# A graph network on one core: the attention's last 1130 targets move from matrix products to gathered rows

## The chip, the cores and the metric

The kernel runs on one core of a Trainium2 chip. A core has five engines that work beside each other and take their instructions in order, each from its own queue: PE (TensorE, matrix products), DVE (VectorE), ACT (ScalarE), POOL (GpSimd) and SP (SyncE, which here only issues DMAs). GpSimd also issues DMAs, the indirect ones, in which a list of row numbers says which rows of a table come in. The metric is the device time of one launch in microseconds (us), lower is better; the figure for a kernel is the median of its runs.

## The reference

Four layers act on 6250 nodes of 128 features and 206,250 edges; each layer's output is added to its input and normalised over the features. `src` and `dst` are the ends of an edge, and the edges are sorted by `dst`.

```python
x = layernorm(x + L0(x))   # x @ Ws.T + bs + mean over a node's edges of x[src] @ Wn.T + bn
x = layernorm(x + L1(x))   # relu([x[src], edge_attr] @ W1 + b1) @ W2 + b2, mean per dst, then a two-layer MLP per node
x = layernorm(x + L2(x))   # x_comb = [x, sum of edge_attr @ We + be]; x_comb + sum of x_comb[src]; a two-layer MLP
x = layernorm(x + L3(x))   # attention, below
# L3, with 4 heads of 32 features and n = 6250; a loop edge from each node to itself is added
h = (x @ W).reshape(n, 4, 32)
a_src, a_dst = (h * att_src).sum(-1), (h * att_dst).sum(-1)
e = exp(leaky_relu(a_src[src] + a_dst[dst], 0.2) - max over the edges of dst)
out = segment_sum(h[src] * e[..., None], dst) / segment_sum(e, dst)
x3 = relu(layernorm(out.reshape(n, 128) + bias, gamma, beta))
```

## The kernel before

Nodes are held 128 to a partition block: `NB` = 49 blocks, the last of 106 rows. `groups` are the 13 runs of up to four blocks (512 nodes, the last of 106), `duos` the 25 runs of two. The program is written out in one order by hand (a manual schedule): each engine executes its instructions in the order in which the Python code issues them, so a generator that is advanced step by step (`yield`) puts its pieces between those of the main loop. There are four stages.

**dense0** makes the adjacency matrix. For two blocks of targets at a time, GpSimd gathers each target's stretch of the sorted edge list: 64 slots of `dst` and of `src` (`search`, `find`, lines 831 to 860). `sort` (line 862) marks the slots whose `dst` is the target itself (`mine`). DVE compares them with counters (`onehots`, line 891, bf16), PE multiplies the comparisons, and the counts go to `A` and from there to a table `adj` in DRAM (line 1007), for all later stages. `prepare_chunks` (line 275) loads all of `src` and `dst` into `src_i` and `dst_r`, 147 chunks of 128 x 11 edges that stay in SBUF.

**mlp** (line 1054) runs layer 1 over the edges, 441 units of up to 4 x 128 edges. For each, SP loads edge features (line 1069), GpSimd gathers the rows of `t1` by columns of `src_i` (line 127 by way of line 1073), PE multiplies (lines 1093 and 1107), and `onehot` (line 782) compares `dst_r` with a counter once a chunk.

**dense2** (line 1012) does layer 2 with `adj`, 25 rounds of 147 products. SP loads each round's piece of `adj` in five DMAs (line 1027) as buffers come free. `node2` (line 494), advanced by one step every ten products, finishes a duo of the round before: it leaves the projected features `hs` in `acc` and the attention's two scalars per node and head in `al`.

**attend** (line 1134) does layer 3 as products with `adj` too. exp of a leaky ReLU of a sum is one of two products of a factor per source and a factor per target, and a comparison chooses which. The 13 groups make six `units`: five of two groups (1024 targets), and a sixth of two groups plus the last 106 targets (`more`, lines 1147 to 1149). For each head and unit a loop of 25 iterations passes over the sources, two blocks an iteration: 4 x 6 x 25 = 600 iterations. In an iteration SP loads the piece of `adj` that is needed three iterations later (line 1283), ACT makes the comparison `r` for two blocks (line 1320), DVE takes `B = min(A, r)` and `C = A - B` in bf16 (lines 1327 and 1329), and PE adds ten products of 512 columns to the sums (line 1347). The sixth unit also has the products of line 1349, and the DVE operations of lines 1333 and 1334, for its 106 extra targets.

Around the loop, lanes advance generators. A `Lane` (line 1253) lets one generator take a step at every second iteration: `sums` closes the last unit (`close`, line 1224) and transposes the next unit's targets; `ends` normalises and stores finished groups in the last head (`finish3`, line 615); `news` makes the next head's source tables (`tables`, line 1185) from the second unit of a head on. `tables` splits an f32 into three bf16 parts: ACT copies (line 1196), GpSimd subtracts (line 1198), ACT copies the rest, GpSimd subtracts again, ACT copies. For the first head the same is done in the first unit, two groups ahead of need.

Of the kernel before, what the change touches and what calls it, by code (L numbers as in the profile page):

```python
# [9 lines left out]
F32 = mybir.dt.float32  # L10
BF16 = mybir.dt.bfloat16
I32 = mybir.dt.int32
# [6 lines left out]
P = 128  # L19
# [49 lines left out]
def kernel(  # L69
# [38 lines left out]
    dram = ctx.enter_context(tc.tile_pool(name="dram", bufs=1, space=bass.MemoryType.DRAM))  # L108
    setup = ctx.enter_context(ExitStack())
# [8 lines left out]
    t3 = dram.tile([N, HW], F32)  # L118
    t3d = dram.tile([N + W, 2 * HEADS], F32)
# [24 lines left out]
    src_i = const.tile([P, NCH, T], I32)  # L144
    dst_r = const.tile([P, NCH, T], F32)
# [128 lines left out]

    def prepare_chunks(prep, pps):

        dst_i = dst_r.bitcast(I32)
        nc.vector.memset(src_i[:, NCH - 1, :], 0)
        nc.vector.memset(dst_i[:, NCH - 1, :], -1)
        for to, of in ((dst_i, dst), (src_i, src)):  # L280
            if NF:
                nc.sync.dma_start(to[:, :NF, :], of[: NF * P * T].rearrange("(c p t) -> p c t", p=P, t=T))
            if tail:
                nc.sync.dma_start(to[:tail, NF, :], of[NF * P * T :].rearrange("(p t) -> p t", t=T))
# [25 lines left out]
        nc.vector.tensor_sub(dst_r, dst_r, w0b.unsqueeze(2).to_broadcast([P, NCH, T]))  # L310
# [183 lines left out]
    def node2(acc, al, pool, pps, n0, rows, nb, G=4, hT=None):  # L494
# [32 lines left out]
        if not keep:  # L527
            nc.vector.tensor_copy(hs[:rows, :nb, D:], al[:rows, 0, b0 : b0 + nb, :])
            store(t3, hs, n0, rows, nb)
# [103 lines left out]
    def general():  # L633
        with ExitStack() as st:
            gp = st.enter_context(tc.tile_pool(name="gacc", bufs=1))
            acc = gp.tile([P, 3, NA], F32, name="gacc")
            for k in range(3):
# [4 lines left out]
                           allow_small_or_imprecise_dtypes=True)  # L642
            row_i = gp.tile([P, NCH], I32, name="row_i")
# [3 lines left out]
            def edges(name, rows_of):  # L647
                with tc.tile_pool(name=f"{name}s", bufs=1) as ep, \
# [5 lines left out]
                    nc.vector.tensor_copy(node, dst_r[:, ds(c, 1), :].rearrange("p c t -> p (c t)"))  # L654
                    w0 = ep.tile([P, 1], F32, name="w0")
                    nc.vector.tensor_copy(w0, w0b[:, ds(c, 1)])
                    ri = ep.tile([P, 1], I32, name="ri")
                    nc.vector.tensor_copy(ri, row_i[:, ds(c, 1)])
                    nc.vector.tensor_scalar(node, node, w0, None, op0=ALU.add)
# [96 lines left out]
    def fast():  # L756
# [24 lines left out]

        def onehot(ep, c, bufs=2):
            K = sizes[c]
            oh = ep.tile([P, T, W], F32, name="oh", bufs=bufs)
            nc.vector.tensor_tensor(
                oh[:K], iota[:K, :W].unsqueeze(1).to_broadcast([K, T, W]),
                dst_r[:K, c, :].unsqueeze(2).to_broadcast([K, T, W]), ALU.is_equal)
            return oh
# [11 lines left out]
        def dense0(stack):  # L800
# [21 lines left out]
            with tc.tile_pool(name="d0o", bufs=1) as one, tc.tile_pool(name="d0", bufs=1) as ep, \  # L822
# [39 lines left out]
                def sort(sb):  # L862
# [5 lines left out]
                    nc.vector.tensor_reduce(degc[:, 2 * sb : 2 * sb + 2], mine, AX.X, ALU.add)  # L868
                    low = ep.tile([P, 2, S], I32, name="low")
# [94 lines left out]
                for sb in range(NS + 1):  # L964
# [5 lines left out]
                    for i in range(STEPS):  # L970
                        g = sb * STEPS + i
                        if g == 2:
                            flush_dma(nc.sync)

# [79 lines left out]
        def mlp(name, node, pool, pps):  # L1054
# [4 lines left out]
            with tc.tile_pool(name=f"{name}e", bufs=1) as ep, \  # L1059
# [5 lines left out]
                def load(i):  # L1065
# [5 lines left out]
                    g[i] = ep.tile([P, U, H], F32, name="g1", bufs=AHEAD + 1)  # L1071
                    for t in range(k):
                        gather(g[i][:K, t, :], t1, src_i[:, c, :], a + t, K)
# [60 lines left out]
        def attend(acc, al):  # L1134


            M = 3 * (CH + 1)
# [8 lines left out]

            units = [(g[0][0], g, []) for g in (groups[k : k + 2] for k in range(0, len(groups), 2))]
            if len(units) > 1 and len(units[-1][1]) == 1 and units[-1][1][0][2] == 1:
                units[-2][2].extend(units.pop()[1])
            with tc.tile_pool(name="f3c", bufs=1) as one, tc.tile_pool(name="f3", bufs=2) as ep, \  # L1150
# [22 lines left out]
                s = one.tile([P, NB, HEADS], F32, name="s")  # L1173
# [3 lines left out]
                nc.scalar.activation(vs, vs, AF.Exp)  # L1177

# [28 lines left out]
                def targets(k, h, n0, of, more):  # L1207

                    to = one.tile([P, 2 * F + P], F32, name=f"ad{k % 2}")
                    last = None  # L1210
                    for m0, rows, nb in of + more:
# [12 lines left out]
                def close(h, of, s):  # L1224

                    sT = []
                    for (m0, rows, nb), sums in zip(of, s):
                        sT.append(ep.tile([M, 2, F], F32, name="sT") if rows * nb > P else one.tile([M, 2, P], F32, name="sTm"))
                        nc.scalar.copy(sT[-1][:, 0, : rows * nb], sums[0])
# [22 lines left out]

                class Lane:


                    def __init__(self):
                        self.left, self.due = [], 0
# [4 lines left out]
                    def step(self, now):  # L1262
                        if self.left and now >= self.due:
# [3 lines left out]
                            self.due = now if lag is self else now + (lag or 2)  # L1267
# [5 lines left out]
                A, more_of, ready = {}, {}, {}  # L1273
                steps = [(h, *u) for h in range(HEADS) for u in units]
                work = [(h, n0, of, more, a) for h, n0, of, more in steps for a in range(0, NB, 2)]

                def load(i):
                    if i < len(work):
                        h, n0, of, more, a = work[i]
# [5 lines left out]
                        if more:  # L1285
                            more_of[i] = ep.tile([P, 2, 2 * P], BF16, name="Am", bufs=4)
                            nc.sync.dma_start(more_of[i][:, :n].rearrange("p l q -> p (l q)"),
                                              adj[more[0][0] // (2 * P), :, a * 2 * P : (a + n) * 2 * P])

                sums, news, ends = Lane(), Lane(), Lane()  # L1290
# [3 lines left out]
                first = [tables(0, groups[k::2]) for k in range(2)]  # L1294
                made, i, now = 0, 0, 0
                for k, (h, n0, of, more) in enumerate(steps):
                    ad, n, m = ready.pop(k), width(of), width(more)
                    tab, minus = tabs[h % 2]
                    s = [[sps.tile([P, F], F32, name="s") for g in of] for _ in range(2)]
                    sm = rps.tile([P, 2, P], F32, name="sm") if more else None  # L1300
# [9 lines left out]
                    for b in range(0, NB, 2):  # L1310
# [5 lines left out]
                        At, Am = A.pop(i), more_of.pop(i, None)  # L1316
                        i += 1
                        r = ep.tile([P, 2, 2 * F + P], BF16, name="r")
                        for l in range(kk):
                            nc.scalar.activation(r[:, l, : n + m], ad[:, : n + m], AF.Relu,  # L1320
                                                 bias=bias[:, b + l, h : h + 1], scale=BIG)
# [9 lines left out]
                        if more:  # L1331
                            bm = ep.tile([P, 3, P], BF16, name="Bm")
                            nc.vector.tensor_tensor(bm[:, :kk, :m], Am[:, :kk, :m], r[:, :kk, n : n + m], ALU.min)
                            nc.vector.tensor_sub(bm[:, 2, :m], Am[:, 0, :m], bm[:, 0, :m])
                        terms = [(0, tab[:, b, 0], lambda c0, c1: bt[:, 0, c0:c1], lambda: bm[:, 0, :m])]
                        if kk == 2:
                            terms += [
                                (0, tab[:, b + 1, 0], lambda c0, c1: bt[:, 1, c0:c1], lambda: bm[:, 1, :m]),
                                (1, minus[:, b // 2], lambda c0, c1: bt[:, 1, c0:c1], lambda: bm[:, 1, :m]),
                                (1, tab[:, b + 1, 1], lambda c0, c1: At[:, c0 // w : c1 // w, 1, :w], lambda: Am[:, 1, :m])]  # L1340
                        terms.append((1, tab[:, b, 1], lambda c0, c1: ct[:, c0:c1], lambda: bm[:, 2, :m]))
# [75 lines left out]
```

## Time and profile before

| | |
|---|---|
| median of 3 runs | 4996.36 us (4988.17 to 5003.37) |
| the profiled execution's own time | 5474.87 us, of which the span is 5473.1 us |
| mean granted TensorE clock in it | 0.942 |
| busy in the span: PE, DVE, ACT, POOL | 91%, 55%, 47%, 36% |
| first attention product of line 1347 to the last | 3886 to 5407 us of the span |
| 0 to 848 us, GpSimd's first gather of layer 1 | dense0, at 848.7 us |
| layer 1's gathers | 848.7 to 3396 us, 1617 of them |

The profile is of one execution, which took 9.6% longer than the median; times in it are compared with its own span. "Busy" counts the time in which an engine executes; a busy PE is not PE at its peak, and pieces of work on one engine overlap a little. The page's second part cuts the span into 40 slices of 137 us, one digit each, in tenths. In a group's row the columns are: source line, engine, operation, output and inputs, their shapes, the count, the busy time in us, the mean of one in ns, and the idle time before them with what ended it. A row of the timeline has the start in us, the duration in us, the engine, the line, and the idle time before it in brackets.

### The profile page before, as it was taken

The numbers are of one execution on the slowest core, as the hardware profiler recorded it, in microseconds if no ns is written. First come the engines' busy times: TensorE is split into PE (matmuls) and PEld (weight loads), VectorE is DVE, ScalarE is ACT, GpSimd is POOL, SyncE is SP. The second block draws the span as 40 slices with busy tenths as digits, with TensorE's granted clock in tenths as the row PEclk, the third lists the DMA queues.
The fourth block names the chain that finished last, engine by engine and source line by source line (L and its number), as shares of the span: only waits on it lengthen the run. The fifth ranks groups of instructions, "written<-read, shape, count | busy, mean of one in ns | idle before, by whom it ended". The sixth has DMA issues, their size and how long they took to land. (4 is left out here: it accounts for less than half of the span.)

```text
span 5473.1 us, 90752 instructions
## 1 busy us (share of the span) xinstructions
PE 4978.6 (91%) x33855; PEld 4095.8 (75%) x33855; DVE 3007.3 (55%) x5084; ACT 2592.4 (47%) x3617; POOL 1989.4 (36%) x1966
## 2 busy tenths in 40 slices
PE   4999998998998999988999999999699999999995
PEld 3999997887888888888888888899455555555553
DVE  6888873233333333332333333222488888888998
ACT  3444442233323333332323323100599899999884
POOL 3333325666666666666666665000110010010000
PEclk9999998899998998998998988999899999999997
DMA  6333324444444444444444443555377777777773
GB/s 120 121 133 133 139 114 137 125 128 126 126 125 124 123 124 125 125 126 124 127 124 126 128 125 99 191 187 188 115 216 217 220 217 226 215 214 227 211 212 116
DMA packets 599589, 834.35 MB, mean 152 GB/s; under 512 B 119837, under 2 KB 484313, under 8 KB 594917
## 3 DMA queue, kind: packets, MB, share of 16 engines
q1 hardware_dynamic: 513077, 603.59, 36.3%
q0 software_dynamic: 85072, 224.21, 14.3%
q8 instruction: 272, 4.46, 0.3%
q14 instruction: 176, 1.44, 0.1%
q10 hardware_dynamic: 992, 0.66, 0.1%
HBM read 738.23 MB, written 89.88 MB: 151 GB/s over the span
## 5 line engine op out<-in xcount | busy, mean ns | idle before, releaser
L127 POOL DMA_INDIRECT g<-t,src_i x1617 | 1570.4, 971 | 986.8 <-issue 785.7
L1320 ACT ACTIVATE r<-ad,bias 128x1024 bf16<-128x1024 f32 (+1 forms) x1176 | 1276.7, 1155 | 91.6 <-DVE B L1327 57.6
L1095 DVE TENSOR_TENSOR g<-g,pre 128x512 f32<-128x512 f32 x882 | 548.0, 640 | 1320.3 <-issue 339.6
L1347 PEld LDWEIGHTS <-acc 128*99 128x99 bf16 x5856 | 698.1, 126 | 606.7 <-issue 157.7
L1107 PE MATMUL seg<-oh,g 128*128 128x64 f32 (+1 forms) x6468 | 1036.5, 284 | 44.4 <-issue 42.2
L1107 PEld LDWEIGHTS seg<-oh,g 128*128 128x128 f32 (+1 forms) x6468 | 959.3, 205 | 82.4 <-issue 48.6
L1093 PE MATMUL pre<-W1s,eaT 128*128 128x256 f32 (+1 forms) x3234 | 892.5, 417 | 115.5 <-DVE g L1095 57.3
L1347 PE MATMUL s<-B,acc 128*99 128x512 bf16 x3504 | 885.4, 382 | 89.4 <-DVE B L1327 84.0
L1096 ACT ACTIVATE g<-g 128x512 f32<-128x512 f32 x882 | 506.2, 592 | 681.8 <-DVE g L1095 478.9
L1093 PEld LDWEIGHTS pre<-W1s,eaT 128*128 128x128 f32 (+1 forms) x3234 | 634.8, 209 | 244.9 <-issue 110.6
L1327 DVE TENSOR_TENSOR B<-A,r 128x2048 bf16<-128x2048 bf16 x600 | 723.2, 1205 | 119.8 <-ACT r L1320 90.6
L1084 ACT COPY eaT<-tp 128x512 f32<-128x512 f32 (+1 forms) x441 | 240.7, 546 | 1067.7 <-PE pre L1093 316.5
L1107 PE MATMUL seg<-oh,ea 128*128 128x64 f32 (+1 forms) x3234 | 664.7, 287 | 32.2 <-issue 31.3
L1107 PEld LDWEIGHTS seg<-oh,ea 128*128 128x128 f32 (+1 forms) x3234 | 528.3, 204 | 32.8 <-issue 32.2
L907 ACT CAST A<-pa 128x784 bf16<-128x784 f32 x400 | 324.5, 811 | 349.2 <-PE pa L904 320.3
L798 PE MATMUL sum<-A,xs 128*128 128x256 bf16 (+1 forms) x3675 | 467.5, 273 | 0.4 <-ACT A L907 0.4
L1329 DVE TENSOR_TENSOR C<-A,B 128x1024 bf16<-128x1024 bf16 x600 | 430.4, 717 | 63.6 <-PE s L1347 0.8
L1198 POOL TENSOR_TENSOR xs<-xs,acc 128x264 f32<-128x264 f32 (+1 forms) x104 | 103.7, 1004 | 993.6 <-ACT acc L1196 972.3
L798 PE MATMUL sum<-A,acc 128*128 128x256 bf16 (+1 forms) x3675 | 409.4, 271 | 3.5 <-DMA A<-adj 3.5
L798 PEld LDWEIGHTS <-acc 128*128 128x128 bf16 x3675 | 355.2, 98 | 45.0 <-issue 5.0
L798 PEld LDWEIGHTS <-xs 128*128 128x128 bf16 x3675 | 357.6, 102 | 35.3 <-issue 0.6
L904 PE MATMUL pa<-oh,oh 128*128 128x98 bf16 x3200 | 355.8, 269 | 28.0 <-ACT A L907 23.4
(229 smaller groups left out, 4472.7 us busy)
## 6 DMA issues: line engine op xcount, KB each, us to landing
A<-adj SPq DMA_DIRECT2D x2304, 128.0 KB
ea<-in_edge_attr_dram SPq DMA_DIRECT2D x292, 256.0 KB
A<-adj SPq DMA_DIRECT2D x100, 704.0 KB
ea<-in_edge_attr_dram SPq DMA_DIRECT2D x146, 192.0 KB
g<-t,src_i POOLq DMA_INDIRECT x1617
Am<-adj SPq DMA_DIRECT2D x96, 128.0 KB
A<-adj SPq DMA_DIRECT2D x25, 320.0 KB
t<-y SPq DMA_DIRECT2D x24, 256.0 KB
```

The costliest lines, as they stand in the source:

```text
L127: nc.gpsimd.indirect_dma_start(out=to, out_offset=None, in_=table, in_offset=bass.IndirectOffsetOnAxis(ap=index[:K, t : t + 1], axis=0))
L798: nc.tensor.matmul(ps[:, :n], parts[part][:, b, :], a(b)[:, :n], start=k == 0, stop=k == 3 * NB - 1)
L904: nc.tensor.matmul(ps[:, o, q * LO : (q + 1) * LO], ohs[g][0][:, 2 * j + o, :, q], ohs[g][1][:, 2 * j + o, :, q], start=True, stop=True)
L907: nc.scalar.copy(A[sb][:, :, q0 : q0 + 2 * QI].rearrange("p k (o q) -> p k o q", q=QI), ps[:, :, : QI * LO].rearrange("p o (q k) -> p k o ...
L1093: nc.tensor.matmul(pre[:K, t, :], eaT[i][:, b + t, :K], W1s[:, 1, :], start=True, stop=True)
L1095: nc.vector.tensor_add(gb, gb, pre[:K, :n, :])
L1096: nc.scalar.activation(gb, gb, AF.Relu)
L1107: nc.tensor.matmul(ps[:, m, :], rows, oh[c][:K, a + t, :], start=a + t == 0 and m == 0, stop=a + t == T - 1, skip_group_check=True)
L1320: nc.scalar.activation(r[:, l, : n + m], ad[:, : n + m], AF.Relu, bias=bias[:, b + l, h : h + 1], scale=BIG)
L1327: nc.vector.tensor_tensor(wide(bt), At[:, :ns, :kk, :w], wide(r), ALU.min)
L1329: nc.vector.tensor_sub(ct[:, :n].rearrange("p (s q) -> p s q", q=w), At[:, :ns, 0, :w], bt[:, 0, :n].rearrange("p (s q) -> p s q", q=w))
L1347: nc.tensor.matmul(s[to][g][:M, : c1 - c0], row, rhs(c0, c1), start=to not in begun, stop=stop)
```

## The change

The attention's matrix part keeps five units (`UNITS`), the first 5120 targets: 4 x 5 x 25 = 500 iterations. The last three groups (`rest`: 512, 512 and 106 targets, nine blocks) are worked out from their slots. Four things are done for it, in this order of the program:

- dense0's `sort` writes each such block's masked source numbers and the mask to DRAM (`slot_src`, `slot_not`), five times two DMAs.
- `src` and `dst` no longer stay in SBUF for layer 1. `load_edges` brings a chunk's two columns in two small DMAs on SP's queue, six chunks ahead; `onehot` subtracts the chunk's first node first (`at`). `prepare_chunks` still loads all of `dst` for its own use, not `src`.
- `node2` in dense2 stores `hs` and the source scalar to a table `t3` of 132 columns, two DMAs a duo on SP's queue.
- `attend` gets a generator `gathered` in a lane `others`, which takes a step at every iteration. It works through 72 chunks of eight slots of one block: GpSimd gathers eight times 128 rows of `t3`, three chunks ahead of need (four buffers); then, a step each, DVE forms the logits, ACT takes exp, DVE multiplies the rows by it, and PE adds the eight slots into one PSUM tile with the identity as weights. An absent slot has 300 taken from its logit. After eight chunks DVE divides.

The sixth unit, `more` and its operations are gone. The general path, which another branch would take for other inputs, is adapted and not run here.

```diff
@@ dense0, sort
                     nc.vector.tensor_reduce(degc[:, 2 * sb : 2 * sb + 2], mine, AX.X, ALU.add)
+                    if 2 * sb + 2 > R0:
+                        k0 = 2 * sb - R0 // 2 * 2
+                        of = ep.tile([P, 2, S], I32, name="of")
+                        nc.vector.tensor_tensor(of, s, mine, ALU.mult)
+                        nc.sync.dma_start(slot_src[k0 : k0 + 2].rearrange("b p s -> p b s"), of)
+                        none = ep.tile([P, 2, S], F32, name="none")
+                        nc.vector.tensor_scalar(none, mine, -1.0, 1.0, op0=ALU.mult, op1=ALU.add)
+                        nc.sync.dma_start(slot_not[k0 : k0 + 2].rearrange("b p s -> p b s"), none)
@@ fast
+        def load_edges(c):
+
+            if c < NCH:
+                edges[c] = edge_pool.tile([P, 2, T], I32, name="edges", bufs=8)
+                for k, of in enumerate((src, dst)):
+                    nc.sync.dma_start(edges[c][: sizes[c], k, :],
+                                      of[c * P * T : c * P * T + sizes[c] * T].rearrange("(p t) -> p t", t=T))
+
         def onehot(ep, c, bufs=2):
             K = sizes[c]
+            at = ep.tile([P, T], F32, name="at", bufs=2)
+            nc.vector.tensor_scalar(at[:K], edges.pop(c)[:K, 1, :], w0b[:K, c : c + 1], None, op0=ALU.subtract)
@@ mlp, load
                     g[i] = ep.tile([P, U, H], F32, name="g1", bufs=AHEAD + 1)
+                    if a == 0:
+                        load_edges(c + 6)
                     for t in range(k):
-                        gather(g[i][:K, t, :], t1, src_i[:, c, :], a + t, K)
+                        gather(g[i][:K, t, :], t1, edges[c][:, 0, :], a + t, K)
@@ node2
-        if not keep:
+        if keep:
+            for c, of in ((slice(0, D), hs), (slice(D, HW), al[:, 0, b0 : b0 + nb, :])):
+                nc.sync.dma_start(t3[n0 : n0 + n, c].rearrange("(b p) d -> p b d", p=rows), of[:rows, :nb])
+        else:
@@ attend
-            units = [(g[0][0], g, []) for g in (groups[k : k + 2] for k in range(0, len(groups), 2))]
-            if len(units) > 1 and len(units[-1][1]) == 1 and units[-1][1][0][2] == 1:
-                units[-2][2].extend(units.pop()[1])
+            units = [(groups[2 * k][0], groups[2 * k : 2 * k + 2]) for k in range(UNITS)]
...
+                def gathered():
+
+                    Q = 8
+                    chunks = [(g, j, q) for g, (n0, rows, nb) in enumerate(rest) for j in range(nb) for q in range(0, S, Q)]
+                    rows_of, slots = {}, {}
+
+                    def issue(i):
+                        if i < len(chunks):
+                            g, j, q = chunks[i]
+                            if q == 0:
+                                k = rest[g][0] // P + j - R0 // 2 * 2
+                                slots[g, j] = [ep.tile([P, S], dt, name=name) for dt, name in ((I32, "slot"), (F32, "none"))]
+                                for t, of in zip(slots[g, j], (slot_src, slot_not)):
+                                    nc.sync.dma_start(t, of[k])
+                            rows_of[i] = ep.tile([P, Q, HW], F32, name="g3", bufs=4)
+                            for t in range(Q):
+                                gather(rows_of[i][:, t, :], t3, slots[g, j][0], q + t, P)
+
+                    for i in range(3):
+                        issue(i)
+                    yield 8
+                    for i, (g, j, q) in enumerate(chunks):
+                        issue(i + 3)
...
+                        if q == 0:
...
+                            ps = rps.tile([P, HW], F32, name="sg")
+                            nc.tensor.matmul(ps, ident, own, start=True, stop=False)
+                            yield
+                        nc.vector.tensor_add(e, e, al[:, 1, b].unsqueeze(1).to_broadcast([P, Q, HEADS]))
+                        nc.vector.scalar_tensor_tensor(e, e, SLOPE, e, op0=ALU.mult, op1=ALU.max)
+                        nc.vector.tensor_sub(e, e, less[:, q : q + Q])
+                        yield
+                        nc.scalar.activation(e, e, AF.Exp)
+                        yield
+                        xh = x[:, :, :D].rearrange("p t (h c) -> p t h c", h=HEADS)
+                        nc.vector.tensor_mul(xh, xh, e.unsqueeze(3).to_broadcast([P, Q, HEADS, CH]))
+                        yield
+                        for t in range(Q):
+                            nc.tensor.matmul(ps, ident, x[:, t, :], start=False, stop=q + t == S - 1)
+                        yield
+                        if q + Q == S:
...
+                            if j == nb - 1:
+                                ends.add(finish3(go, pool, n0, rows, nb))
+                            yield
...
-                sums, news, ends = Lane(), Lane(), Lane()
+                sums, news, ends, others = Lane(), Lane(), Lane(), Lane(1)
...
+                others.add(gathered())
...
-                        if more:
-                            bm = ep.tile([P, 3, P], BF16, name="Bm")
-                            nc.vector.tensor_tensor(bm[:, :kk, :m], Am[:, :kk, :m], r[:, :kk, n : n + m], ALU.min)
-                            nc.vector.tensor_sub(bm[:, 2, :m], Am[:, 0, :m], bm[:, 0, :m])
...
-                        for lane in (sums, news, ends):
+                        for lane in (sums, news, ends, others):
                             lane.step(now)
```

## The prediction

> **What bounds the kernel now.** I read the page's slices first, for the stages, then busy time and groups in the attention, then single instructions.
>
> ```profile
> PE   4999998998998999988999999999699999999995
> DVE  6888873233333333332333333222488888888998
> ACT  3444442233323333332323323100599899999884
> POOL 3333325666666666666666665000110010010000
> ```
> ```profile
> 3903.00:5407.00 1504.00, 1423.30 (x7228) 859.95 (x7228) 1321.55 (x1983) 1348.28 (x1424) 96.07 (x92) 0.99 0.72 213
> ```
>
> The last 11 slices are the attention. The second row is its main part, 3903 to 5407 us: stretch and sum, then PE, PEld, DVE, ACT and POOL busy, the granted clock (0.99), DMA share, GB/s. PE is busy 95% of it, ACT 90%, DVE 88%, GpSimd 6%: three engines share the bound, and GpSimd alone is free. In layer 1 (slices 6 to 24) PE is the bound and GpSimd is at 6 tenths with its gathers.
>
> ```profile
> L1320 ACT ACTIVATE r<-ad,bias 128x1024 bf16<-128x1024 f32 (+1 forms) x1176 | 1276.7, 1155 | 91.6 <-DVE B L1327 57.6
> L1347 PE MATMUL s<-B,acc 128*99 128x512 bf16 x3504 | 885.4, 382 | 89.4 <-DVE B L1327 84.0
> L1327 DVE TENSOR_TENSOR B<-A,r 128x2048 bf16<-128x2048 bf16 x600 | 723.2, 1205 | 119.8 <-ACT r L1320 90.6
> L1329 DVE TENSOR_TENSOR C<-A,B 128x1024 bf16<-128x1024 bf16 x600 | 430.4, 717 | 63.6 <-PE s L1347 0.8
> L1198 POOL TENSOR_TENSOR xs<-xs,acc 128x264 f32<-128x264 f32 (+1 forms) x104 | 103.7, 1004 | 993.6 <-ACT acc L1196 972.3
> ```
>
> Each engine waits only for its neighbour: shortening one helps little, leaving out iterations helps all. By the ACT copies of line 1229 that end each unit, a unit of 1024 targets takes 60.3 us (25 iterations of 2.41), the sixth 67.2, 67.4, 67.1 and in the last head 73.4.
>
> GpSimd's gathers come in no attention row of before, so two other places price them: layer 1, where they run back to back, and dense0, where DVE does long bf16 operations beside them. Timelines of GpSimd, then DVE, then GpSimd in dense0:
>
> ```profile
> 2001.04 0.95 POOL L127 DMA_INDIRECT g<-t,src_i  x1 [0.30 <-issue]
> 2002.30 0.95 POOL L127 DMA_INDIRECT g<-t,src_i  x1 [0.30 <-issue]
> ```
> ```profile
> 316.82 2.28 DVE L891 TENSOR_TENSOR oh<-kp,table 128x4096 bf16<-128x4096 bf16 x1
> 319.03 1.78 DVE L891 TENSOR_TENSOR oh<-kb,table 128x3136 bf16<-128x3136 bf16 x1
> ```
> ```profile
> 316.38 0.96 POOL L127 DMA_INDIRECT sup<-in_dst_dram,at  x1 [0.15 <-DVE low L870]
> 317.64 2.28 POOL L127 DMA_INDIRECT sup<-in_dst_dram,at  x1 [0.30 <-issue]
> 320.23 1.40 POOL L127 DMA_INDIRECT slots<-in_dst_dram,at  x1 [0.30 <-issue]
> ```
>
> Free, a gather takes 0.95 us plus a gap of 0.30: one per 1.25 us, of rows of 256, 1024 or 1500 bytes alike. Beside L891 it takes 2.28: it began at 317.64, DVE's operation ended at 319.10, and it ended 0.82 later, though DVE's next operation began at once. The third likewise ends 0.82 after 320.81. So a gather waits out the DVE operation that it meets, and no more.
>
> **What is removed.** Four sixth units, 67.2 + 67.4 + 67.1 + 73.4 = 275 us, with all they do on PE, ACT, DVE and SP. Attention before, from the first product (3886) to the last (5407): 1521 us.
>
> **What the new lane costs the three engines.** A chunk takes four steps, and two more for each eight chunks, so 4.25 iterations; with the first wait of eight iterations the lane is through after 8 + 72 x 4.25 = 314 of 500. PE, a chunk: eight f32 products of 132 columns. The layer-1 product of line 1093 (256 columns) comes as two records 0.216 us apart, that of line 1107 (64 columns) as two 0.112 apart; 132 columns lie near the lower, 8 x 2 x 0.112 = 1.8 us. Bounds: 0 if they fell into PE's 5% of idle time, 8 x 2 x 0.216 = 3.5. DVE: the product of 1024 f32 elements, 1.2 us (line 439's 128x1024 f32 takes 1.16), three small operations of 0.17 (line 1193), a share of the block's own: 1.8 us. ACT: one exp of 32 elements, 0.25. On engines alone a chunk takes 4.25 x 2.41 + 1.8 = 12.0 us. This is on the path.
>
> **What it costs GpSimd: the step that decides.** Eight gathers a chunk are 10.0 us free, and would hide in 12.0. But DVE is seldom idle here. In a chunk it does 4.25 times B (1.22 us in this stage) and C (0.70), and the 1.2 us product. An arrival at a random time meets an operation of length d with chance d/T and waits d/2: (4.25 x (1.22^2 + 0.70^2) + 1.2^2)/2 = 4.9, so 4.9/T us a gather, T being the chunk's time. L1198 gives the same picture: 0.67 us when free, 1.0 in the mean. T = 8 x (1.25 + 4.9/T) gives T = 13.0 us, and a gather every 1.63 us. So GpSimd, not PE, sets the pace, by 1 us a chunk.
>
> [...] I take 13.0, and keep 12.0 as the lower end.
>
> `tables` adds to it: its subtracts stand in the same queue. In the changed kernel's instruction order eight gathers lie ahead of nearly each pair. While a next head's tables are made (100 of 125 iterations), every eight iterations (1.88 chunks) bring two subtracts of 1.14 us: 1.2 us a chunk. ACT's next copy waits for the subtract, 2 x 2.41 = 4.8 us after it was issued, while eight gathers of 1.5 take 12: ACT stands some 7 us, behind it the comparisons `r`, DVE and PE. That is no loss of its own while GpSimd stays busy through it: three chunks are in hand, so DVE has its rows when ACT goes on. I allow GpSimd 0.4 us of idling a chunk: T = 11.6 + 8 x 4.9/T, T = 14.35 us.
>
> **The sum for the attention.** The first unit took 86 us (3886 to 3972), its subtracts in bursts 15 us apart. Now 24 gathers come first, 35 us, of which a burst's 15 are free: +20. Four rounds of eight gathers and four subtracts take 12 + 5 where they took 15: +8. In all 114 us, with 7 chunks gathered. Of the other 65, 50 iterations without tables hold 12, at 13.0 = 156; 53 at 14.35 = 761. The last three chunks' products: 5. By then 300 iterations are done; 200 remain, x 2.41 = 482, and 15 for the last head, whose units before took 62 to 65 us beside `finish3`. Sum: 114 + 156 + 761 + 5 + 482 + 15 = 1533, +12 on 1521.
>
> **The rest.** Tail: before, DVE finished six groups after the last product, at 9.2 us each (line 618 begins at 5416.37 and 5425.56), because `ends` takes 17.5 iterations a group. Now three groups are finished early; in the last head 100 iterations remain after its first unit, some 5.3 groups, so 4.7 are left where 5 full ones and a small one were: -9. Attention's head: a handful of DVE operations and an exp: +2. dense2: SP's queue now has two stores between a round's five loads and the next five, and they wait for `al`. DVE's line 525 ends it at 3622.9 in the round from 3610.9 to 3628.1, so all five loads wait until 5.2 us before need. Two 704 KB loads issued at 3614.9 had landed by 3618.7; the first tile should just come in time. Bounds 0 and 25 x 2 us; taken +3. Layer 1: two loads of 128 runs of 44 bytes a chunk, six chunks ahead; SP takes 0.4 us to issue each in 16, and `at` is 0.17 us on a DVE a third busy, so nothing, hidden by five units of prefetch; if a gather's index were late, PE would be next. Bounds 0 and 40. dense0: ten small DVE operations and DMAs against a load of all `src` saved, nothing.
>
> +12 - 9 + 2 + 3 = +8 us on 5473, +0.15%. The median is 0.913 of the profiled execution's 5474.87; +7 on 4996.36 gives **5004**.
>
> **Rivals.**
>
> - GpSimd keeps up (gathers free as in layer 1, or met between operations). Then 65 chunks at 12.0 = 780 replace 917, and the start is 105: 1387 in place of 1521, with the rest -138, -126 on the median: 4870. For it: GpSimd is 6% busy now. Against: dense0's rows.
> - Slower: ACT's stalls aren't covered. Each subtract of `tables` after the first head's holds ACT, and GpSimd runs dry meanwhile, because the next gathers are issued only as the lanes move on. Eight iterations then take 8 x 2.41 + 1.88 x 1.8 + 2 x 7 = 36.7 us where the sum has 27. With 5 us uncovered a stall: 32.7, times 28 such stretches: +160, so +168 and 5150. It decides against the change from about 2 us a stall. For it: 993.6 us of L1198's idle time ended by ACT shows how tight this chain is. Against: three chunks in hand.
> - The stages before pay: small loads delay layer 1 by 40 us or dense2 by 2 us a round. With the attention level, 5040. Against: no DMA is waited for long there now.
>
> **How the numbers follow.** About 0.3%, 15 us, is what can be told from no change. GpSimd sets the pace as summed: 0.45, its own range 4955 to 5050 (0.08 us a gather, from a chunk's 13.0 or 14.35 being 0.65 out, is 46 us); of it 0.15 faster, 0.11 same, 0.19 slower. GpSimd keeps up: 0.20. ACT stalls: 0.26. Earlier stages: 0.09, 0.01 of it the same. Faster 0.35, same 0.12, slower 0.53. The range, 4855 to 5140, reaches into both outer cases.
>
> **What would show it.** Gathers of the attention at 1.25 us in the mean with their gap: the first rival. At 1.5 to 1.7, with GpSimd near 90% busy for a thousand us: the sum. ACT's line 1196 copies waiting for `xs` over 5 us, with GpSimd idle just after: the second rival. Round length 17.2 us in dense2 and layer 1's 2548 us unchanged: the rest right. If f32 products of 132 columns cost more than 0.25 us, or the new loads stop SP, the prediction is wrong by something that I don't see.

## The result, and the profile after

The changed kernel takes 5191.4 us in the median of four runs (5185.31 to 5199.07), the kernel before 4995.49 in the median of four. The ratio is 1.0393, with an interval of 1.0371 to 1.0415: slower by 3.9%. The forecast was 5004, its range 4855 to 5140.

The profile of before that is shown above has to be set right first. That execution's span was 5473.1 us because its layer 1 was long: its gathers ran from 848.7 to 3396 us, and the granted clock was 0.91 from 1000 to 2800 us. In another profiled execution of the same kernel (span 4989.6, below called "before, second profile") they end at 2928, the clock there is 1.00, and the attention is as long as it was: first product at 3403.1, last at 4923.5, 1520.5 us. After the change layer 1's gathers run from 852 to 2928 us. One group of the runs below came from a chip where layer 1 took some 2570 us in each kernel profiled, where the kernel before took 5485 us, and where engines stood idle here and there with no cause in the profile; those runs are compared with each other only.

By stage, in us of the span:

| | before, second profile | after |
|---|---|---|
| layer 1, first gather to last | 2078 | 2076 |
| first attention product at | 3403.1 | 3408.7 |
| attention, first product to last | 1520.5 | 1720.1 |
| last product to the end | 66.0 | 54.5 |

So the attention lost 199.6 us, the tail gave 11.5 back, and what lies ahead cost 5.6. All of the loss is in the attention. Its slices, after (slices of 130 us, the attention from slice 27 on):

```profile
PE   4999998999999999999999999947878777779995
DVE  6888875344444444444444322246667756678898
ACT  4444443333333333333333210045556655569985
POOL 3343333777777777777777400045656665541000
PEclk9999999999999999999999999978889988989998
```

Windows of the attention of after, then of the second profile of before (stretch and sum, PE, PEld, DVE, ACT, POOL busy, granted clock, DMA share, GB/s):

```profile
3425.00:5128.00 1703.00, 1372.23 (x6758) 862.68 (x6758) 1205.80 (x1889) 1147.09 (x1296) 732.59 (x659) 0.92 0.75 173
```
```profile
3420.00:4923.00 1503.00, 1422.78 (x7227) 862.00 (x7227) 1321.70 (x1983) 1347.68 (x1423) 96.84 (x92) 0.99 0.71 213
```

Before, PE was busy 95% of this stretch, ACT 90%, DVE 88%. After, it is 81%, 67% and 71%, and GpSimd has 43%. No engine is full any more: the loss is waiting, not work. (In the rows of after the lines have moved: `r` is 1423, PE's products 1444, `B` 1429, `C` 1431, the subtract of `tables` 1241 and ACT's copy 1239, the gather's helper 135; in edited kernels they shift by two more at most.) The DMA share rises while the bytes moved per second fall, from 213 to 173. That pair is the first hint that some transfers have become dear. The groups, after:

```profile
L1423 ACT ACTIVATE r<-ad,bias 128x1024 bf16<-128x1024 f32 x980 | 1050.7, 1137 | 140.7 <-DVE B L1429 140.2
L1444 PE MATMUL s<-B,acc 128*99 128x512 bf16 x2920 | 771.6, 402 | 345.6 <-DVE B L1429 341.7 <-ACT sT L1272 1.7
L135 POOL DMA_INDIRECT g<-t,slot x576 | 673.1, 1169 | 451.0 <-issue 185.1 <-PE sg L1348 103.6 <-PE s L1444 56.1
L1429 DVE TENSOR_TENSOR B<-A,r 128x2048 bf16<-128x2048 bf16 (+1 forms) x500 | 603.7, 1207 | 435.4 <-ACT r L1423 237.0 <-DMA A<-adj 154.7 <-PE s L1444 23.9
L1431 DVE TENSOR_TENSOR C<-A,B 128x1024 bf16<-128x1024 bf16 x500 | 352.0, 704 | 52.7 <-PE s L1444 0.9 <-PE sg L1348 0.5 <-DVE B L1429 0.5
L1241 POOL TENSOR_TENSOR xs<-xs,acc 128x264 f32<-128x264 f32 (+1 forms) x104 | 80.7, 784 | 231.6 <-ACT acc L1239 209.1 <-DMA slot<-slot_src 21.7
```

`B` on DVE (line 1429) waited 120 us in all before and 435 now, and the row names the two things that end these waits: ACT's comparisons `r`, 237 us, and the loads of `adj`, 155 us. The gathers themselves are not the bound: they have 451 us of idle time, of which 185 are the gaps of 0.3 us between them. The waits from 3540 to 4450 us, where most of the gathering lies (called "the stretch" from here on; us in all, times, longest):

```profile
ACT acc L1239 <- POOL xs L1241: 200.2, 33, 13.8
PE s L1444 <- DVE B L1429: 192.8, 73, 11.5
...
DVE B L1429 <- ACT r L1423: 141.1, 47, 10.9
DVE B L1429 <- DMA A<-adj: 106.0, 33, 11.5
```

The chain reads from the top: ACT waits 33 times, 6 us each, for a GpSimd subtract of `tables`; its comparisons come late by as much, so DVE waits for `r`, and PE for DVE. Beside this runs a second chain: 33 times DVE waits for a piece of `adj`, 3.2 us each. In the same stretch of the second profile of before there were five such waits, 3.4 us together.

One place shows both. The timelines of GpSimd, ACT, DVE and PE of after (start, duration, idle time before it in brackets):

```profile
3656.33 0.68 POOL L1241 TENSOR_TENSOR xs<-xs,acc 128x264 f32<-128x264 f32 x1
...
3668.56 0.94 POOL L135 DMA_INDIRECT g<-t,slot  x1 [1.05 <-DMA g<-t,slot]
3669.51 0.68 POOL L1241 TENSOR_TENSOR xs<-xs,acc 128x264 f32<-128x264 f32 x1
3681.64 0.96 POOL L135 DMA_INDIRECT g<-t,slot  x1 [11.45 <-issue]
```
```profile
3657.04 0.42 ACT L1239 CAST acc<-xs 128x264 bf16<-128x264 f32 x1 [7.72 <-POOL xs L1241]
3657.37 2.18 ACT L1423 ACTIVATE r<-ad,bias 128x1024 bf16<-128x1024 f32 x2
```
```profile
3672.27 1.23 DVE L1429 TENSOR_TENSOR B<-A,r 128x2048 bf16<-128x2048 bf16 x1 [5.80 <-DMA A<-adj]
...
3682.87 1.29 DVE L1429 TENSOR_TENSOR B<-A,r 128x2048 bf16<-128x2048 bf16 x1 [7.37 <-DMA A<-adj]
```
```profile
3673.55 2.72 PE L1444 MATMUL s<-B,acc 128*99 128x512 bf16 x6 [4.81 <-DVE B L1429]
...
3677.77 2.13 PE L1348 MATMUL sg<-g,ident 128*128 128x132 f32 x16
3684.22 2.06 PE L1444 MATMUL s<-B,acc 128*99 128x512 bf16 x6 [4.32 <-DVE B L1429]
...
3688.49 1.46 PE L1444 MATMUL s<-B,acc 128*99 128x512 bf16 x6
```

ACT stood 7.72 us until the subtract at 3656.33 was through, and only then made its next comparisons. Then DVE stood 5.80 and 7.37 us for two loads. While everything stood, GpSimd stood too: its next gather began at 3681.64, after 11.45 us. That fits its buffer, one of four, coming free only when line 1348 had read it, at 3677.77 + 2.13 = 3679.90. And PE, after 4.81 us of idling, took 2.72 us for six products that take 1.46 in a full stream; more on that in the last section.

### The profile page after: what moved, and what is told of

It reads as the page before. It is cut to its first block, busy times and chain, and to the rows that moved or that the text cites. A ratio compares the mean times of both kernels' runs of the same rounds, so it can differ in the third digit from the quotient of the medians.

```text
span 5183.3 us, 90914 instructions
## 1 busy us (share of the span) xinstructions
PE 4660.0 (90%) x33381; PEld 3920.8 (76%) x33381; DVE 2933.1 (57%) x5116; ACT 2394.5 (46%) x3478; POOL 2653.6 (51%) x2542
## 3 DMA queue, kind: packets, MB, share of 16 engines
q0 software_dynamic: 103504, 263.17, 23.1%
q14 instruction: 186, 1.52, 0.1%
## 5 line engine op out<-in xcount | busy, mean ns | idle before, releaser
L135 POOL DMA_INDIRECT g<-t,edges x1617 | 1584.8, 980 | 502.7 <-issue 391.1
L1444 PEld LDWEIGHTS <-acc 128*99 128x99 bf16 x4880 | 639.9, 132 | 839.2 <-issue 467.7
L1423 ACT ACTIVATE r<-ad,bias 128x1024 bf16<-128x1024 f32 x980 | 1050.7, 1137 | 140.7 <-DVE B L1429 140.2
L1444 PE MATMUL s<-B,acc 128*99 128x512 bf16 x2920 | 771.6, 402 | 345.6 <-DVE B L1429 341.7
L1143 PE MATMUL seg<-oh,g 128*128 128x64 f32 (+1 forms) x6468 | 964.1, 272 | 0.0
L1143 PEld LDWEIGHTS seg<-oh,g 128*128 128x128 f32 (+1 forms) x6468 | 887.8, 192 | 24.0 <-issue 1.2
L135 POOL DMA_INDIRECT g<-t,slot x576 | 673.1, 1169 | 451.0 <-issue 185.1
L1429 DVE TENSOR_TENSOR B<-A,r 128x2048 bf16<-128x2048 bf16 (+1 forms) x500 | 603.7, 1207 | 435.4 <-ACT r L1423 237.0
L1129 PE MATMUL pre<-W1s,eaT 128*128 128x256 f32 (+1 forms) x3234 | 776.7, 381 | 20.2 <-DVE g L1131 20.2
L1431 DVE TENSOR_TENSOR C<-A,B 128x1024 bf16<-128x1024 bf16 x500 | 352.0, 704 | 52.7 <-PE s L1444 0.9
```

What stands on the lines that cost most here:

```text
L135: nc.gpsimd.indirect_dma_start(out=to, out_offset=None, in_=table, in_offset=bass.IndirectOffsetOnAxis(ap=index[:K, t : t + 1], axis=0))
L1129: nc.tensor.matmul(pre[:K, t, :], eaT[i][:, b + t, :K], W1s[:, 1, :], start=True, stop=True)
L1143: nc.tensor.matmul(ps[:, m, :], rows, oh[c][:K, a + t, :], start=a + t == 0 and m == 0, stop=a + t == T - 1, skip_group_check=True)
L1423: nc.scalar.activation(r[:, l, :n], ad[:, :n], AF.Relu, bias=bias[:, b + l, h : h + 1], scale=BIG)
L1429: nc.vector.tensor_tensor(wide(bt), At[:, :ns, :kk, :w], wide(r), ALU.min)
L1431: nc.vector.tensor_sub(ct[:, :n].rearrange("p (s q) -> p s q", q=w), At[:, :ns, 0, :w], bt[:, 0, :n].rearrange("p (s q) -> p s q", q=w))
```

## The experiments

The runs were made on several chips. Beside the first three runs the kernel before took 4999.36 us, beside the last four 4995.87, so their times are set against the 5191.4 of after; the four between them are of the chip with the long layer 1.

Two causes were to be told apart. **The queue**: `tables`' subtracts stand behind gathers in GpSimd's queue, ACT waits for them, and all wait for ACT. **The row**: absent slots have the source number 0, since `of = s * mine`, so most of the later gathers of a block fetch one row of `t3` again and again; if such packets are slow, the loads of `adj` come late behind them. The mean degree is 33 and a block has 64 slots, so the last three or four of its eight chunks are nearly all absent. The trace keeps every packet of the DMA queues; the mean of the gathers' packets (eight rows, 4224 bytes), by chunk of a block, is this in after:

```
chunk      1     2     3     4     5     6     7     8
us      0.292 0.301 0.298 0.323 0.621 1.213 1.331 1.238
```

Up to the degree a packet takes 0.30 us, beyond it four times as much.

**Absent slots keep the number of their neighbour in the edge list**

```diff
-                        of = ep.tile([P, 2, S], I32, name="of")
-                        nc.vector.tensor_tensor(of, s, mine, ALU.mult)
-                        nc.sync.dma_start(slot_src[k0 : k0 + 2].rearrange("b p s -> p b s"), of)
+                        nc.sync.dma_start(slot_src[k0 : k0 + 2].rearrange("b p s -> p b s"), s)
```

The logits of these slots have 300 taken off as before, so the same is computed.

> The changed kernel, but absent slots keep the source number that stands in the edge list there (some other target's) in place of 0; the mask takes them out as before. Hot row: all absent slots name row 0 of the table, and packets of the slots from 40 on take 1.2 us where those of the first 32 take 0.30; the loads of the adjacency wait their turn behind them. Then these packets fall to 0.30 us, units with gathers take 76 to 85 us in place of 100, the attention falls from 1720 to 1530 to 1560 us and the time from 5191 to about 5000 to 5035 us. ACT's stalls behind GpSimd (the second rival of the prediction): packets get shorter, the units do not: 5150 to 5191 us.

It took 5069.01 us, ratio 1.0149 (1.0130 to 1.0168), so 122 us less than after. The attention took 1605 us. Packets now take 0.28 to 0.31 us in all eight chunks. Their share of the DMA engines' time, after and then here, for the same count and bytes (packets, MB, share):

```profile
q0 software_dynamic: 103504, 263.17, 23.1%
```
```profile
q0 software_dynamic: 103504, 263.17, 18.9%
```

The waits here, in the same stretch:

```profile
ACT acc L1237 <- POOL xs L1239: 213.4, 30, 14.5
...
DVE B L1427 <- DMA A<-adj: 7.5, 5, 6.5
```

The waits for `adj` fall from 106.0 to 7.5 us. Nothing in the attention but the numbers of the absent rows was changed, so the row is a cause. That it acts by late loads can be read from the packets too. `adj`'s own packets (1024 bytes) take 0.054 us in the mean of the stretch in after and 0.052 here, so they are not slower; they come later. From the issue of a load to the end of its last packet pass 2.6 us in the median and 6.9 or more for a tenth of the loads in after, and 2.2 and 2.8 here (an estimate: packets are counted off in the order of the issue, 128 a load). ACT's waits for the subtracts stay as they were: 30 of 7.1 us. The gain is short of what was expected, as the second cause is still there.

**`tables`' subtracts on DVE**

```diff
-                                nc.gpsimd.tensor_sub(xs[:, :nb], xs[:, :nb], tab[:, bs, :, k, :])
+                                nc.vector.tensor_sub(xs[:, :nb], xs[:, :nb], tab[:, bs, :, k, :])
```

> The changed kernel with the subtracts of the source tables on VectorE in place of GpSimd. ACT's stalls behind GpSimd: the nine units with tables and gathers fall from 100 us to the 76 of the one unit without tables, so 9 x 20 = 180 us: 5000 to 5030 us. Hot row: the adjacency loads stay late, the waits only move to them, and at most a quarter of the 199 us comes back: 5140 to 5190 us.

It took 5073.29 us, ratio 1.0157 (1.0136 to 1.0178): 118 us less than after, the attention 1606 us. The first unit, whose subtracts had 24 gathers ahead of them, takes 93 us where after has 128. Now the other wait is the long one:

```profile
DVE B L1429 <- DMA A<-adj: 163.2, 46, 11.6
```

It grew from 106.0 to 163.2 us: part of the late loads had been hidden behind ACT's waits, as the sum of both edits bears out below.

**One DMA for an iteration's piece of `adj`, in place of four**

```diff
-                        for k in range(-(-width(of) // (2 * P))):
-                            nc.sync.dma_start(A[i][:, k, :n].rearrange("p l q -> p (l q)"),
-                                              adj[sb + k, :, a * 2 * P : (a + n) * 2 * P])
+                        m = -(-width(of) // (2 * P))
+                        nc.sync.dma_start(A[i][:, :m, :n].rearrange("p k l q -> p k (l q)"),
+                                          adj[sb : sb + m, :, a * 2 * P : (a + n) * 2 * P].rearrange("k p q -> p k q"))
```

> The changed kernel with an iteration's adjacency piece (4 x 128 KB) loaded in one DMA in place of four. Depth: each of SP's DMAs waits for the one eight before it to land, so with four an iteration only two iterations' pieces can be under way, and at 8 to 14 us a landing this is what limits; with one DMA all three pieces that have buffers are under way: 5040 to 5110 us. Hot row: each piece still passes behind the same long packets of gathers; 5130 to 5190 us. ACT's stalls: 5191 us.

It took 5149.17 us, ratio 1.0308 (1.0290 to 1.0325): 42 us less, attention 1679. In the stretch DVE's waits for `adj` are 96.7 us, hardly fewer than 106.0; over the whole attention they are 115.7 where after has 154.7, and these 39 us are about the gain. With other row numbers they fall to 11.1. The expected depth of SP's queue is in the trace of after: of the 1966 loads of `adj` with another of them eight places ahead, one was issued before that one had landed (by 0.06 us); for seven places ahead it is 49 of 1967. But landings of 8 us and more are few, 63 of 940 in the stretch (landings by the same estimate as above). So how many loads are under way is the smaller part, a quarter of these waits, and the slow rows are the larger.

**Row 0 in every slot** (the sum over the neighbours is not formed, all slots gather row 0)

```diff
-                        nc.vector.tensor_tensor(of, s, mine, ALU.mult)
+                        nc.vector.tensor_scalar(of, s, 0, None, op0=ALU.mult)
```

> The changed kernel with row 0 in every slot (the output of the gathered targets is then that of row 0, so the sum over neighbours is left out in its sense, not in its work). Hot row: all 64 gathers of a block have packets of 1.2 to 1.3 us, where the changed kernel has them only from slot 32 on, mean 0.70; 576 x 0.55 = 320 us more of each DMA engine, of which about half shows, as in the undoing (0.41 us a packet, 235 us, gave 122): 5310 to 5450 us. If the address doesn't matter and the late slots are slow for another reason, 5191 us.

This and the next three are of the chip with the long layer 1, where the kernel before took 5485.04 us. It took 5852.73, ratio 1.0672 (1.0612 to 1.0732), attention 1891 us, packets 1.0 to 1.4 us in all chunks. DVE's waits for `adj` from 4000 to 5300 us:

```profile
DVE B L1429 <- DMA A<-adj: 320.7, 83, 10.7
```

On this same chip the kernel with both edits (below), whose rows differ, has 2.6 us of such waits from 3980 to 4950, where its gathers lie. So the dose goes with the effect: packets slow in no chunk, and next to no waits; in all chunks, and 320.7 us of them. That late slots are slow for another reason than their row is ruled out, since here the early ones are as slow. The attention's 1891 us are of another chip than after's 1720, so their difference isn't used.

**Both edits, and both with the lane resting at every second step**

```diff
-                            self.due = now if lag is self else now + (lag or self.lag)
+                            self.took = getattr(self, "took", 0) + 1
+                            self.due = now if lag is self else now + (lag or self.lag + (self.took % 2 if self.lag == 1 else 0))
```

> Both edits: absent slots keep a source number of their own, and the subtracts of the source tables are on VectorE. If the two causes are separate (rows of one address before the adjacency loads, and ACT behind GpSimd's queue), the gains of 122 and 118 us add up to 240: 4950 us, units with gathers at 76 us or less. If they are two names of one queue, the second gain is small once the first is had: 5030 to 5070 us.

> Both edits, and the lane of the gathered targets rests at every second step, so that its 306 steps spread over 467 of the 500 iterations in place of 314. If GpSimd's pace (eight gathers at 1.25 us and their waits for VectorE) still limits the iterations with gathers, spreading hides it: chunks come every 6.4 iterations or 16 us, well over GpSimd's 13, and what is left is TensorE's 1.8 us a chunk, 130 us on 500 x 2.41: attention 1400 to 1440 us and 4880 to 4920 us. If TensorE and VectorE limit them already, it is level with both edits alone.

> As the last, with each iteration's adjacency piece in one DMA. With the long packets gone and the gathers spread, the loads should be in time as they are: no more than 15 us better, 4870 to 4920 us. If it gains 30 us or more, SP's depth still limits.

Both edits took 5468.63 us, ratio 0.9973 (0.9957 to 0.9989), attention 1504; with rests 5367.48, ratio 0.9784 (0.9744 to 0.9825), attention 1393; with rests and one DMA 5363.96, ratio 0.9782 (0.9740 to 0.9824), attention 1387. By these alone one would say that the two gains add, leave 1504 us, and that GpSimd's pace holds the rest. So the kernel was run on an ordinary chip, beside one that takes the gathers away.

**The same on another chip, and with no gathers.** In the latter a chunk's eight gathers are one plain DMA of 1024 consecutive rows, so that the sum over the neighbours is not the reference's:

```diff
-                            for t in range(Q):
-                                gather(rows_of[i][:, t, :], t3, slots[g, j][0], q + t, P)
+                            nc.gpsimd.dma_start(rows_of[i], t3[: P * Q].rearrange("(p t) d -> p t d", t=Q))
```

> Own source numbers in the absent slots and the tables' subtracts on VectorE, as measured once where layer 1 took 2577 us. If the two gains add in the attention alone, 1504 us of attention again, and with layer 1 at 2078 us a time of 4965 to 4985 us, ratio 0.993 to 0.999 to the kernel before. If the slow layer 1 had part in it, the attention differs by over 20 us.

> Both causes taken out (own source numbers in the absent slots, the tables' subtracts on VectorE), and a chunk's eight gathers replaced by one plain DMA of 1024 consecutive rows on GpSimd's queue: the same bytes, but not the reference's rows. If GpSimd's pace (1.21 us a gather in the mean plus 0.32, so 12.3 us a chunk, as much as the engines' 12.0) is what keeps the attention of that kernel at 1504 us, it falls to 1385 to 1410 us. If the lane's own operations on DVE, ACT and PE hold it up by the moment at which they come, it stays at 1470 to 1505.

> The same with the lane resting at every second step: attention 1393 us again, the time 4860 to 4885 us, ratio 0.973 to 0.979. Near the 4870 that the prediction's first rival (gathers hidden) gave for the whole change.

Both edits took 4855.86 us, ratio 0.9723 (0.9706 to 0.9740), attention 1392 us: 335 us less than after, and faster than before by 2.8%. With no gathers it is 4848.51, ratio 0.9706 (0.9690 to 0.9722), attention 1388. With rests it is 4852.35, ratio 0.9713 (0.9695 to 0.9731), attention 1375, but its tail is longer, 67 us for 53, since groups are finished later. The windows and groups of both edits:

```profile
3425.00:4800.00 1375.00, 1288.98 (x6759) 831.38 (x6759) 1221.11 (x1981) 1138.17 (x1289) 695.51 (x559) 0.99 0.72 214
```
```profile
L1442 PE MATMUL s<-B,acc 128*99 128x512 bf16 x2920 | 722.6, 382 | 99.4 <-DVE B L1427 95.1 <-ACT sT L1270 1.8
L135 POOL DMA_INDIRECT g<-t,slot x576 | 714.4, 1240 | 224.4 <-issue 148.7 <-DVE xs L1239 23.6 <-PE sg L1346 22.3
L1427 DVE TENSOR_TENSOR B<-A,r 128x2048 bf16<-128x2048 bf16 (+1 forms) x500 | 601.0, 1202 | 76.6 <-ACT r L1421 49.8 <-PE s L1442 14.3 <-DMA A<-adj 3.3
```

and the windows with no gathers:

```profile
3420.00:4789.00 1369.00, 1288.18 (x6755) 831.61 (x6754) 1218.16 (x1979) 1136.51 (x1287) 35.90 (x68) 0.99 0.70 214
```

PE is at 94% again, DVE 89%, and `B` waits 77 us in place of 435. That rows come by 576 gathers and not by 72 plain DMAs costs 4 us of attention. (Both are of one profiled execution each.) So the expectation of 1504 us was wrong and its rival, that the other chip had a part in it, right. A likely reading, not tested, is that this kernel has no slack against that chip's idle gaps, since GpSimd executes gathers or is in the gaps between them for 863 of 915 us, 94%, and that the rests give it some. What is different on that chip isn't settled.

The gains also aren't a sum. Either edit alone leaves some 214 us of loss above 1392 (1605 and 1606), both causes together make 328. So some 100 us were under both at once, and the edit that comes second gains 214 where the first gained 115.

**The lane's rests alone, on the changed kernel**

> The changed kernel with one edit: the lane rests at every second step, so its 306 steps reach over 467 of the 500 iterations. Row 0 in the absent slots and the subtracts behind the gathers stay. If spacing mends only a shortage of GpSimd, which has none here (idle 451 us), the attention stays within 30 us of 1720. If both causes lose by how densely gathers come (longer waits for adjacency loads, and more often a full queue ahead of a subtract), it falls to 1590 to 1660.

It took 5170.02 us, ratio 1.0349 (1.0330 to 1.0368), attention 1693: 27 us less. Spacing the gathers mends neither cause.

## Why the prediction was wrong

**What is removed, and what the chunks cost PE, DVE and ACT: right.** Units without a lane take 60 us before and after. The 12.0 us a chunk are borne out: with both causes gone a unit of 25 iterations (5.88 chunks, 70.6 us by the prediction) takes 68 to 73 us in ten of the twelve that follow the first, and the attention 1392 us where the first rival, "GpSimd keeps up", had 1387. Its 4870 stands against 4855.86 measured with both edits; without the scaling of the last paragraph of this section it would have been 4858.

**GpSimd as the pace: the mechanism right, the bound wrong.** Gathers do wait for DVE's operations: with both edits a quarter take 0.94 us or less, a quarter 1.52 or more, and the mean is 1.24, with the gap 1.54, where the sum had 1.63. The trace of that run shows the wait itself: 294 gathers begin while DVE executes `B`, and they end 0.82 us after it in the median (eight in ten between 0.81 and 0.93), the 0.82 of dense0. So `B` holds a gather up as L891 did, which the prediction had from two gathers of dense0 and applied to `B` and `C` as an estimate. But eight of 1.54 are 12.3 us against the engines' 12.0, not 13.0, and little of that shows: 4 us in all, where the sum had 65 of its 917 - 780 = 137 us for this. (The other 72 are its allowance for the subtracts, which this kernel no longer has in GpSimd's queue.) The first of after's two full units without tables, 76.1 us, seems to say 13.0 a chunk (76.5); but the other takes 96.1. The two take 73.9 and 68.2 us with spread rows, 72.7 and 68.7 with both edits, 72.7 and 69.6 with no gathers.

**`tables`: the step that failed.** "That is no loss of its own while GpSimd stays busy through it: three chunks are in hand, so DVE has its rows when ACT goes on." The 7 us of a stall were right (30 waits of 7.1 with spread rows). The cover was not there. The gathered rows in hand are work for one lane; ACT's comparisons feed every iteration of the main loop, so a stall of ACT stops DVE and PE whatever lies in the buffers. And GpSimd was no bound under which a stall could hide: it too ran dry (11.45 us in the timeline above). This is the second rival, at 0.26; its point of decision, 2 us a stall, was passed. Taken out last it is worth 1605 - 1392 = 213 us. Over the whole attention of the run with spread rows ACT waits 263.5 us for these subtracts, so some four fifths of the waiting showed; the rival had allowed for 5 of 7 us.

**The loads of `adj`: a term that was not in the sum.** The prediction priced the gathers on GpSimd's queue, and none on the DMA engines. Nine blocks x 64 gathers x 16 packets are 9216 packets; at the 0.30 us of an ordinary row they are 2765 us over 16 engines, 173 us, and do no harm (with both edits DVE waits 2.9 us for `adj` in the stretch). At after's mean of 0.70 they are 404. The 231 more agree with the row of the queue (23.1% of 5183 against 18.9% of 5062: 241 us), and come in bunches, three or four chunks of every eight. `adj`'s loads are issued three iterations ahead, 7.2 us at 2.41, and with 6.9 us or more to land for a tenth of them that is no longer enough. The line that should have given the alarm stands in the diff: `s * mine`, with a mean degree of 33 in 64 slots, makes nearly half of all rows one row. Taken out last, it is worth 1606 - 1392 = 214 us. The forecast of 5150 for the second rival thus lies near the 5191 measured for half the reason.

**The first unit.** 114 us were forecast, 128 measured; with the subtracts off GpSimd 93. The cause was named (24 gathers ahead) and its size too small: some 40 us more than the 88 of before, where the forecast had 28 more than 86.

**The rest.** Tail -9 forecast, -11.5 measured. Layer 1 level: -2. Ahead of the attention +5 in all (head, dense2, dense0), measured +5.6; over the runs with the changed stages the first product lies between 3401 and 3412, so this is about its scatter. One reading behind the dense2 term was wrong: in the trace of before one 704 KB load, not two, was issued at 3615.1 and had landed by 3618.7. It did no harm: dense2's 25 rounds take as long as before, but for three that take 0.7 to 1.8 us more. The scaling by 0.913 was wrong in kind: nearly all the surplus of that execution was in layer 1 (470 of 483 us), and a saving in the attention isn't to be scaled. It cost 1 us here, and 12 in the first rival.

## What to carry to other kernels

Padding of index lists should name rows spread over the table, not one: the packets of the masked slots took four times as long here as those of the real ones (1.2 to 1.3 us, and 0.30). Before an engine is taken for free because it is 6% busy, look for what already stands in its queue for the engines that are full: one short operation behind eight gathers held ACT up for 6 us in the mean here, and DVE and PE behind it, and moving it to DVE (0.41 us each) was cheaper than any gather. Price a gather three times: on its queue, on the queue's other users, and on the DMA engines.

## What the runs showed of the hardware

- Packets of eight rows of 528 bytes take 0.30 us where rows differ and 1.2 to 1.3 where nearly all are one row. Why, the runs don't tell: whether one address or one region of memory is slow wasn't tried.
- Stalls of PE cost more than their length in after. After 4.81 us of idling six products took 2.72 us in place of 1.46. Over the attention of after, 360 of 4880 products of line 1444 follow each other at 0.40 to 0.45 us, where the usual is 0.216; with both edits 65 do. The 295 more are some 63 us of PE time (an estimate: 295 times the 0.21 us between the two spacings), and the granted clock is 0.92 where it is 0.99 with both edits. In the timeline above it is 0.50 from 3671.30 to 3678.00, 1.00 from 3678.10 to 3684.90, 0.50 from 3684.95 to 3688.30 and 1.00 from 3688.35 to 3690.00: the six products at 3684.22, after 4.32 us of idling, take 2.06 us, those at 3688.49 again 1.46. By what rule the clock falls and comes back was not shown. How much of the 63 us was on the path no run tells apart.
- A gather of 528-byte rows takes GpSimd 0.94 us when free, as those of 256 to 1500 bytes did.
